# Two heads' score products as two row tiles of 64 in place of products over all 128 partitions, in a conditioned transformer block

## Chip, core and metric

One Trainium2 chip, one of its cores. The metric is the device time of the whole program in microseconds (us), here the median of three runs of the kernel before: 7162.6 us (7159.1 to 7167.75). Lower is better.

## What is computed

A transformer block on x [2, 2048, 576] with 16 heads of 36 features, all in float32. Cut to what matters here:

```python
mod = silu(c) @ w_ada + b_ada                    # six shifts, scales and gates
xn  = _ln(x, 1e-06) * (1 + sc_msa) + sh_msa
q, k, v = (xn @ w_qkv + b_qkv)                   # [2, 2048, 16, 36] each
q = _ln(q, 1e-05, qn_g, qn_b); k = _ln(k, 1e-05, kn_g, kn_b)
attn = softmax(einsum('bqhd,bkhd->bhqk', q, k) * 36 ** -0.5)
o = einsum('bhqk,bkhd->bqhd', attn, v)
x = x + g_msa * (o @ w_proj + b_proj)
x = x + g_mlp * (gelu(xn2 @ w1 + b1) @ w2 + b2)  # xn2: x normed and modulated again
```

## The kernel before, in words

Stages follow one another: modulation; then for each of the two batches `attention_inputs` (norm, q, k, v), `attention` and `projection`; then the MLP for both batches. The change lies in `attention`.

Attention works on pairs of heads. By `by_feature` (L309) four token tiles of a pair are copied by GpSimd into a staging tile (head 0 in columns 0 to 63, head 1 in 64 to 127, 36 of each used, the rest zero or a passing row), transposed by TensorE (L318, into the one PSUM tile `tp`), and written to SBUF by VectorE with gain and bias per partition (L322). So head 0 lies on partitions 0 to 35 and head 1 on 64 to 99. For k one tile `kt` [128, 2048] holds both heads. For q, `by_feature` writes two copies, `qt[:, 0]` with the gains "q0", which are zero on partitions 64 to 127, and `qt[:, 1]` with "q1", which are zero on 0 to 63: a product over all 128 partitions of `kt` and one of these copies is then one head's alone.

There are 64 steps to a pair (4 blocks of 512 queries by 16 key tiles of 128), and in each, in program order:

- **S**, `scores` (L361): for each head a matmul of keys [128] by queries [512] into its own bank of a two-bank PSUM tile `s`; ScalarE's exponential of both banks follows (L368);
- **M**, `largest` (L336), for the next pair: queries [128] by keys [512], again a bank for each head; VectorE reduces it to each query's largest score (L350). These maxima enter the next pair's S as one more row of q (`shifted_q`, L352) against a row of ones in k;
- **V**, `values` (L371), for the step before: two matmuls with 64 columns of v each, whose outputs take partitions 0 to 63 and 64 to 127 of one bank, `acc`.

**T** stands below for a group of four transposes (L318, or L387 in `finish`). Three `s` tiles of two banks, one `acc` and one `tp` fill PSUM's eight banks. Ahead of the loop stands a first round of 64 M alone for pair 0; pair 7's 64 steps have S and V alone. So the two batches hold 896 steps with S, M and V, 128 with S and V, and 128 M by themselves. The preparation of k and q for the pair after next runs in the last block of a pair (L422). The tile framework's scheduler sets each engine's final order from this program order.

In the profile each float32 matmul is two instructions (two passes, each with a weight load): the 2048 matmuls of L364 are 4096 rows.

The lines that the change touches: the gains (L95 to L109), `by_feature` (L309, L322), `prepare` (L332), `largest` (L343), `shifted_q` (L357), `scores` (L364).

## Time and profile before

| | |
|---|---|
| median of 3 runs | 7162.6 us (7159.1, 7162.6, 7167.75) |
| span of the profiled execution | 7159.0 us |
| the fastest run less that span | 0.1 us |
| TensorE busy | 6975.9 us, 97% |
| VectorE, ScalarE, GpSimd busy | 1964.8, 1441.5, 288.0 us |
| first M to last V of each batch, us of the span | 370 to 2844, 3262 to 5734 |
| MLP | from 5897 us to the end |

The profile is one execution. PE is TensorE's matmuls, PEld its weight loads, DVE is VectorE, ACT ScalarE, POOL GpSimd. The end of a matmul in the profile is modelled (a pass of 512 columns is shown as 592 ns while the next one starts 0.43 us after it), so distances between starts are read, not durations. [...]

### The profile page before, as it was taken

Reading aid. Unit: us, or ns where it says so; the run is one execution under the profiler, and the core shown is the slowest. Engines: PE = TensorE matmul, PEld = TensorE weight load, DVE = VectorE, ACT = ScalarE, POOL = GpSimd, SP = SyncE. Lnnn points to the kernel's source line nnn. Section 1 sums busy time; section 2 is a strip of 40 time slices with the busy share of each in tenths; the row PEclk is TensorE's granted clock in tenths of the full one; section 3 lists DMA queues with packets and bytes.
Section 4 is the critical chain, followed back from the end, with each engine's and each line's share of the span. In section 5 each row is a group of like instructions: output and inputs, shape, how many; then the busy total and the mean of one; then the engine's idle time right before and its main releaser. Section 6 shows DMA issues by size and latency. Waiting matters only on the chain.

```text
span 7159.0 us, 47198 instructions
## 1 busy us (share of the span) xinstructions
PE 6975.9 (97%) x20336; PEld 3021.2 (42%) x20336; DVE 1964.8 (27%) x2256; ACT 1441.5 (20%) x1789; POOL 288.0 (4%) x394
## 2 busy tenths in 40 slices
PE   8989999999999999998999999999999969999999
PEld 6643333333333333564333333333333345555555
DVE  3452333323233320346232333323332020000000
ACT  1102222222222223110222222222222311112110
POOL 0100000000000000110000000000000020000000
PEclk9989999999999999998999999999999989999999
DMA  2000000000000000200000000000000040000000
GB/s 94 5 0 0 0 0 0 0 0 0 0 0 0 0 0 21 90 7 0 0 0 0 0 0 0 0 0 0 0 0 0 1 143 14 14 14 14 15 15 10
DMA packets 35394, 83.60 MB, mean 12 GB/s; under 512 B 4833, under 2 KB 4833, under 8 KB 35185
## 3 DMA queue, kind: packets, MB, share of 16 engines
q1 hardware_dynamic: 29936, 61.69, 2.8%
q0 software_dynamic: 5248, 18.90, 0.7%
q8 instruction: 159, 2.61, 0.2%
q14 instruction: 51, 0.41, 0.0%
HBM read 61.68 MB, written 18.89 MB: 11 GB/s over the span
## 4 chain that ended last, share of the span: by engine, by line
PE 94%; issue 3%; DVE 1%; DMA 1%; ACT 0%; SPq 0%; POOL 0%; POOLq 0%; DVEq 0%; ACTq 0%
PE s L364 27%; PE s L343 25%; PE acc L374 14%; PE s L511 8%; PE s L249 7%; PE s L525 6%; PE s L449 3%; PE tp L318 2%; PE tp L209 1%; PE tp L387 0%; PE tp L138 0%; DMA x<-x_dram 0%; DVE qs L322 0%; DVE qt L322 0%; DMA xt<-in_x_dram 0%
## 5 line engine op out<-in xcount | busy, mean ns | idle before, releaser
L350 DVE TENSOR_REDUCE mx<-s 128x2 f32<-128x1024 f32 x1024 | 1255.3, 1226 | 2937.4 <-PE s L343 2937.1
L364 PE MATMUL s<-qs,kt 128*128 128x512 f32 x4096 | 2029.4, 618 | 14.5 <-DVE qs L322 14.5
L343 PE MATMUL s<-kt,qt 128*128 128x512 f32 x4096 | 1910.4, 593 | 1.9 <-issue 1.9
L368 ACT ACTIVATE pt<-s 128x1024 f32<-128x1024 f32 x1024 | 1047.7, 1023 | 3391.0 <-PE s L364 3391.0
L364 PEld LDWEIGHTS s<-qs,kt 128*128 128x128 f32 x4096 | 699.8, 190 | 1219.6 <-issue 1130.8
L343 PEld LDWEIGHTS s<-kt,qt 128*128 128x128 f32 x4096 | 780.3, 191 | 983.1 <-issue 972.6
L374 PE MATMUL acc<-pt,vt 128*64 128x512 f32 x4096 | 1104.4, 618 | 0.3 <-ACT pt L368 0.3
L511 PE MATMUL s<-xnt,w_sb 128*128 128x512 f32 (+1 forms) x1440 | 676.8, 613 | 0.3 <-ACT xnt L217 0.3
L525 PE MATMUL s<-w_sb,ht 128*128 128x288 f32 x2304 | 563.9, 406 | 0.0
L249 PE MATMUL s<-wq,xnt 128*128 128x288 f32 (+1 forms) x1920 | 543.3, 427 | 7.2 <-DMA wq<-in_w_qkv_dram 6.9
L374 PEld LDWEIGHTS acc<-pt,vt 128*64 128x64 f32 x4096 | 202.9, 135 | 741.3 <-issue 737.7
L525 PEld LDWEIGHTS s<-w_sb,ht 128*128 128x128 f32 x2304 | 435.4, 190 | 119.3 <-issue 1.5
L511 PEld LDWEIGHTS s<-xnt,w_sb 128*128 128x128 f32 (+1 forms) x1440 | 247.7, 189 | 421.0 <-issue 387.4
L249 PEld LDWEIGHTS s<-wq,xnt 128*128 128x128 f32 (+1 forms) x1920 | 334.2, 189 | 206.6 <-issue 142.8
L518 ACT ACTIVATE ht<-s,b_sb 128x512 f32<-128x512 f32 x144 | 98.9, 687 | 949.9 <-PE s L511 949.8
L533 DVE TENSOR_TENSOR y<-s,gate 128x576 f32<-128x576 f32 x32 | 24.2, 758 | 604.5 <-PE s L525 604.5
L449 PE MATMUL s<-wp,ott 128*128 128x288 f32 (+1 forms) x640 | 183.3, 429 | 0.7 <-DMA wp<-in_w_proj_dram 0.7
L322 DVE TENSOR_SCALAR qs<-tp,gain_q,bias_q 128x512 f32<-128x512 f32 x128 | 97.9, 806 | 295.9 <-PE tp L318 295.9
L313 POOL COPY stage_m<-qk 128x288 f32<-128x288 f32 x64 | 27.2, 427 | 3477.0 <-PE tp L318 3477.0
L202 DVE TENSOR_SCALAR xn<-x,mv,rstd 128x576 f32<-128x576 f32 x32 | 18.6, 585 | 491.9 <-PE acc L210 491.5
L449 PEld LDWEIGHTS s<-wp,ott 128*128 128x128 f32 (+1 forms) x640 | 113.1, 192 | 62.2 <-issue 39.9
L217 ACT ACTIVATE xnt<-tp,mod 128x128 f32<-128x128 f32 x256 | 99.1, 456 | 55.2 <-PE tp L209 54.9
(86 smaller groups left out, 1606.6 us busy)
## 6 DMA issues: line engine op xcount, KB each, us to landing
xt<-in_x_dram SPq DMA_DIRECT2D x64, 288.0 KB, 3.1
x_dram<-x POOLq DMA_DIRECT2D x32, 288.0 KB, 3.5
x<-x_dram SPq DMA_DIRECT2D x8, 1152.0 KB, 5.8
out_dram<-y POOLq DMA_DIRECT2D x32, 288.0 KB, 2.4
wa<-in_w_ada_dram SPq DMA_DIRECT2D x6, 1152.0 KB, 6.9
wq<-in_w_qkv_dram SPq DMA_DIRECT2D x6, 1152.0 KB, 11.7
w_sb<-in_w_dram SPq DMA_DIRECT2D x3, 1728.0 KB
w_sb<-in_w_dram SPq DMA_DIRECT2D x4, 1152.0 KB, 11.2
```

Of the source, the lines that this page charges most:

```text
L217: nc.scalar.activation(dst[:m, k, :], t4[:, k * P : (k + 1) * P] if k < 4 else t1[:64, :P], AF.Identity, bias=mod[:m, which, k, b : b + 1] ...
L249: nc.tensor.matmul(ps[:, a, :HALF], xnt[:kk, k, :], wq[:kk, k, f0 : f0 + HALF], start=(k == 0), stop=(k == NKC - 1),)
L318: nc.tensor.transpose(tp[:, i * P : (i + 1) * P], st[:, i].rearrange("p h e -> p (h e)"), ident)
L343: nc.tensor.matmul(ps[:, h, :], qts[p, blk][:, h, i * P : (i + 1) * P], kts[p][:, kq * BLK : (kq + 1) * BLK], start=True, stop=True,)
L350: nc.vector.tensor_reduce(maxima[p, blk][:, i, :, kq], ps, AX.X, ALU.max)
L364: nc.tensor.matmul(ps[:, h, :], kts[p][:, kc * P : (kc + 1) * P], qt[:, h, :], start=True, stop=True)
L368: nc.scalar.activation(pt, ps, AF.Exp, scale=SCALE)
L374: nc.tensor.matmul(acc[64 * h : 64 * h + 64, :], vt[:, v0 : v0 + 64], pt[:, h, :], start=(kc == 0), stop=(kc == NT - 1),)
L449: nc.tensor.matmul(ps[:, a, :HALF], ott[:kk, k, :], wp[:kk, k, a * HALF : (a + 1) * HALF], start=(k == 0), stop=(k == NKC - 1),)
L511: nc.tensor.matmul(ps[:, j, :], w1_sb[:kk, k, f * P : (f + 1) * P], xnt[:kk, k, :], start=(k == 0), stop=(k == NKC - 1),)
L518: nc.scalar.activation(ht[:, f, :], ps[:, j, :], AF.Gelu, bias=b1_sb[:, f : f + 1])
L525: nc.tensor.matmul(ps[:, a, :HALF], ht[:, f, i * P : (i + 1) * P], w2_sb[:, f, a * HALF : (a + 1) * HALF], start=(f == 0), stop=(f == NF - 1),
```

## The change

The second, masked copy of q is gone: gains and biases of q are one tile for both heads, like those of k; `by_feature` writes one tile with one VectorE instruction; `qt` and `qs` are [128, 512] in place of [128, 2, 512]. Each score product takes only its head's partitions, 36 (M) or 37 (S) of them from partition 0 or 64, and so uses a row tile of 64 of the matmul array. Number, columns and output banks of the matmuls stay.

```diff
-    for n, g_in, b_in, starts in (
-        ("k", kn_g, kn_b, (0, 64)),
-        ("q0", qn_g, qn_b, (0,)),
-        ("q1", qn_g, qn_b, (64,)),
-    ):
+    for n, g_in, b_in in (("k", kn_g, kn_b), ("q", qn_g, qn_b)):
...
-            def by_feature(n, p, blk, *normed):
+            def by_feature(n, p, blk, dst, g):
...
-                for dst, g in normed:
-                    nc.vector.tensor_scalar(dst, tp, gains[g], biases[g], ALU.mult, ALU.add)
+                nc.vector.tensor_scalar(dst, tp, gains[g], biases[g], ALU.mult, ALU.add)
...
-                    qt = b2p.tile([P, 2, BLK], F32, name="qt", bufs=5)
-                    by_feature("q", p, i - NBLK, (qt[:, 0, :], "q0"), (qt[:, 1, :], "q1"))
+                    qt = b2p.tile([P, BLK], F32, name="qt", bufs=5)
+                    by_feature("q", p, i - NBLK, qt, "q")
...
                 for h in range(2):
+                    r = slice(64 * h, 64 * h + HD)
                     nc.tensor.matmul(
                         ps[:, h, :],
-                        qts[p, blk][:, h, i * P : (i + 1) * P],
-                        kts[p][:, kq * BLK : (kq + 1) * BLK],
+                        qts[p, blk][r, i * P : (i + 1) * P],
+                        kts[p][r, kq * BLK : (kq + 1) * BLK],
...
-                qt = b2p.tile([P, 2, BLK], F32, name="qs")
-                by_feature("m", p, qb, (qt[:, 0, :], "q0"), (qt[:, 1, :], "q1"))
+                qt = b2p.tile([P, BLK], F32, name="qs")
+                by_feature("m", p, qb, qt, "q")
...
                 for h in range(2):
+                    r = slice(64 * h, 64 * h + HV)
                     nc.tensor.matmul(
-                        ps[:, h, :], kts[p][:, kc * P : (kc + 1) * P], qt[:, h, :], start=True, stop=True
+                        ps[:, h, :], kts[p][r, kc * P : (kc + 1) * P], qt[r, :], start=True, stop=True
                     )
```

Two places where the order of instructions moves. The first is VectorE at the start of a pair's second and third block (qs is the shifted q, L350 and L345 are the reductions behind M, L392 and L388 end `finish`). Before:

```order
L350 TENSOR_REDUCE mx<-s 128x2 x15
L322 TENSOR_SCALAR qs<-tp,gain_q_88,bias_q_89 128x512
L322 TENSOR_SCALAR qs<-tp,gain_q_95,bias_q_96 128x512
L354 TENSOR_REDUCE stage_m_1524<-mx 128x8
L350 TENSOR_REDUCE mx<-s 128x2
L390 RECIPROCAL inv<-tp 128x8
L392 TENSOR_TENSOR qk<-tp,inv 128x4x72
```

With the change:

```order
L345 TENSOR_REDUCE mx<-s 128x2 x15
L316 TENSOR_SCALAR qs<-tp,gain_q,bias_q 128x512
L349 TENSOR_REDUCE stage_m_1516<-mx 128x8
L345 TENSOR_REDUCE mx<-s 128x2
L386 RECIPROCAL inv<-tp 128x8
L388 TENSOR_TENSOR qk<-tp,inv 128x4x72
```

One of the two instructions that write qs is gone, and the others keep their order. The second place is TensorE at the start of the first round, where T for q and M alone alternate. Before:

```order
L318 MATMUL tp<-ident,stage_q_1520 128x128 x4
L343 MATMUL s<-kt,qt 128x512
L318 MATMUL tp<-ident,stage_q_1522 128x128 x4
L343 MATMUL s<-kt,qt 128x512 x3
L318 MATMUL tp<-ident,stage_q_1520 128x128 x4
L343 MATMUL s<-kt,qt 128x512 x4
L318 MATMUL tp<-ident,stage_q_1522 128x128 x4
L343 MATMUL s<-kt,qt 128x512 x120
```

With the change:

```order
L313 MATMUL tp<-ident,stage_q_1512 128x128 x4
L313 MATMUL tp<-ident,stage_q_1514 128x128 x4
L338 MATMUL s<-kt,qt 128x512 x2
L313 MATMUL tp<-ident,stage_q_1512 128x128 x4
L338 MATMUL s<-kt,qt 128x512 x2
L313 MATMUL tp<-ident,stage_q_1514 128x128 x4
L338 MATMUL s<-kt,qt 128x512 x124
```

A few M stand behind a T instead of ahead of it. Elsewhere TensorE's order of S, M, V and T is the one before.

## Rows read from the trace of the kernel before

**Rows 1.** The page: busy time, and the chain that ended last by engine and line

```profile
PE 6975.9 (97%) x20336; PEld 3021.2 (42%) x20336; DVE 1964.8 (27%) x2256; ACT 1441.5 (20%) x1789; POOL 288.0 (4%) x394
...
PE 94%; issue 3%; DVE 1%; DMA 1%; ACT 0%; SPq 0%; POOL 0%; POOLq 0%; DVEq 0%; ACTq 0%
PE s L364 27%; PE s L343 25%; PE acc L374 14%; PE s L511 8%; PE s L249 7%; PE s L525 6%; PE s L449 3%; PE tp L318 2%; PE tp L209 1%; PE tp L387 0%; PE tp L138 0%; DMA x<-x_dram 0%; DVE qs L322 0%; DVE qt L322 0%; DMA xt<-in_x_dram 0%
```

**Rows 2.** The page: groups of attention (count | busy us, mean ns | idle before, releaser)

```profile
L350 DVE TENSOR_REDUCE mx<-s 128x2 f32<-128x1024 f32 x1024 | 1255.3, 1226 | 2937.4 <-PE s L343 2937.1
L364 PE MATMUL s<-qs,kt 128*128 128x512 f32 x4096 | 2029.4, 618 | 14.5 <-DVE qs L322 14.5
L343 PE MATMUL s<-kt,qt 128*128 128x512 f32 x4096 | 1910.4, 593 | 1.9 <-issue 1.9
L368 ACT ACTIVATE pt<-s 128x1024 f32<-128x1024 f32 x1024 | 1047.7, 1023 | 3391.0 <-PE s L364 3391.0
...
L374 PE MATMUL acc<-pt,vt 128*64 128x512 f32 x4096 | 1104.4, 618 | 0.3 <-ACT pt L368 0.3
```

**Rows 3.** Timeline, weight loads of one step (start us, us, engine line op)

```profile
2002.47 0.20 PEld L374 LDWEIGHTS acc<-pt,vt 128*64 128x64 f32 x4 [0.76 <-issue]
2003.48 0.30 PEld L364 LDWEIGHTS s<-qs,kt 128*128 128x128 f32 x2 [0.81 <-issue]
2004.01 0.19 PEld L364 LDWEIGHTS s<-qs,kt 128*128 128x128 f32 x1 [0.24 <-issue]
...
2005.30 0.19 PEld L343 LDWEIGHTS s<-kt,qt 128*128 128x128 f32 x1 [0.24 <-issue]
...
2007.11 0.20 PEld L374 LDWEIGHTS acc<-pt,vt 128*64 128x64 f32 x4 [0.76 <-issue]
```

**Rows 4.** Timeline, weight loads of the MLP around a chunk of 64 rows

```profile
5903.61 0.29 PEld L511 LDWEIGHTS s<-xnt,w_sb 64*128 64x128 f32 x2 [0.76 <-issue]
5904.66 0.30 PEld L511 LDWEIGHTS s<-xnt,w_sb 128*128 128x128 f32 x2 [0.76 <-issue]
5905.20 0.19 PEld L511 LDWEIGHTS s<-xnt,w_sb 128*128 128x128 f32 x1 [0.24 <-issue]
```

**Rows 5.** Timeline, TensorE where T stands between M and S

```profile
1657.95 0.60 PE L387 MATMUL tp<-ident,ot 128*128 128x128 f32 x4
1658.39 1.88 PE L364 MATMUL s<-qs,kt 128*128 128x512 f32 x4
1660.11 0.59 PE L343 MATMUL s<-kt,qt 128*128 128x512 f32 x1
```

**Rows 6.** Timeline, ScalarE and VectorE in the step of rows 3

```profile
2005.56 1.02 ACT L368 ACTIVATE pt<-s 128x1024 f32<-128x1024 f32 x1 [3.62 <-PE s L364]
...
2007.22 1.23 DVE L350 TENSOR_REDUCE mx<-s 128x2 f32<-128x1024 f32 x1 [3.42 <-PE s L343]
```

**Rows 7.** Timeline, VectorE in batch 0's first round

```profile
380.07 2.52 DVE L350 TENSOR_REDUCE mx<-s 128x2 f32<-128x1024 f32 x2
...
386.95 1.23 DVE L350 TENSOR_REDUCE mx<-s 128x2 f32<-128x1024 f32 x1 [0.49 <-PE s L343]
...
395.54 1.23 DVE L350 TENSOR_REDUCE mx<-s 128x2 f32<-128x1024 f32 x1 [0.49 <-PE s L343]
```

**Rows 8.** Timeline, preparation of pair 1 behind that round

```profile
490.08 1.09 PE L318 MATMUL tp<-ident,stage_k 128*128 128x128 f32 x4 [1.00 <-DVE kt L322]
491.20 0.81 DVE L322 TENSOR_SCALAR kt<-tp,gain_k,bias_k 128x512 f32<-128x512 f32 x1 [1.27 <-PE tp L318]
...
493.22 1.53 DVE L322 TENSOR_SCALAR qt<-tp,gain_q,bias_q 128x512 f32<-128x512 f32 x2 [1.21 <-PE tp L318]
...
496.02 1.53 DVE L322 TENSOR_SCALAR qt<-tp,gain_q,bias_q 128x512 f32<-128x512 f32 x2 [1.27 <-PE tp L318]
```

**Rows 9.** Busy time by stretch: pair 1 and pair 7 of batch 0

```profile
812.30:1120.20 307.90, 305.29 (x832) 111.94 (x833) 96.69 (x96) 67.83 (x68) 5.13 (x12) 0.99 0.00 0
2652.00:2843.60 191.60, 190.53 (x538) 59.56 (x538) 8.30 (x16) 67.24 (x67) 0.85 (x2) 0.99 0.00 0
```

## The prediction

> **What bounds the kernel now.** The page comes first: TensorE is busy for 97% of the span and holds 94% of the chain that ended last; of that chain the two score products hold 27% (S) and 25% (M), and V 14% [rows 1]. VectorE and ScalarE wait for TensorE: before the 1024 reductions behind M VectorE is idle for 2937 us, before the exponentials ScalarE for 3391 us, while S waits 14.5 us in all and M and V almost nothing [rows 2]. So a step costs what TensorE needs for it.

> What it needs is read from the starts of the weight loads of one step [rows 3]. S starts at 2003.48, M at 2005.30, the next V at 2007.11; V had started at 2002.47. V takes 1.01 us, S 1.82, M 1.81, together 4.64 us. In the first round, where M runs alone, reductions start every (395.54 - 386.95) / 5 = 1.718 us for four passes [rows 7]; that is 0.43 us a pass, one slot below. So S is four slots and 0.10, M four and 0.09. V has four passes too, but takes 1.01 us, two slots (0.86) and 0.15: the four loads of both heads begin within 0.20 us (the row reads 0.20 us for x4), and the passes run two at a time, each head in its own 64 columns of the array. V shows that two float32 products in different parts of the array run side by side here, and that the second pass of one head does not hold up the first of the other.

> The fractions over are the price of changing the shape of the tile. [...] The same price stands at the MLP's chunk of 64 rows, the one place where a row tile of 64 already runs: two passes there take 5904.66 - 5903.61 = 1.05 us in place of 0.86, 0.19 over, and again 0.11 behind the return (5905.20 - 5904.66 = 0.54) [rows 4]. I take 0.20 us a change. Between T and S, both of 128 rows and columns, there is none: T takes 0.44 us, and S behind it 1.72, four bare slots [rows 5].

> **The change part by part.**

> *Full steps.* With head 0 in rows 0 to 63 and head 1 in rows 64 to 127, S and M run as V does, if row tiles behave as column tiles: eight passes in four slots. Each of the 896 full steps loses 4 x 0.4295 = 1.718 us, from 4.64 to 2.92; V and the two changes of shape stay. 896 x 1.718 = 1539 us.

> *Pair 7.* 128 steps of S and V lose two slots: 128 x 0.859 = 110 us. Its 64 steps now take 191.6 us a batch [rows 9].

> *First round.* M alone would fall from 1.718 to 0.859, but VectorE's reduction takes 1.23, and two in a row 2.52 us, so 2.52 - 1.23 = 1.29 from start to start [rows 7]. VectorE is late next: 1.718 - 1.29 = 0.43 gained for each of about 120 M (four in each batch stand among the T): 52 us. Were TensorE still the bound it would be 110.

> *VectorE.* The second copy of q goes: one instruction of 0.81 in place of two in 1.53 us [rows 8]. In the loop this is hidden before and after. In the preparation ahead of the loop TensorE waits for VectorE, groups of q follow every 496.02 - 493.22 = 2.80 us, and would follow 0.72 sooner: four groups in each batch for certain, some more in front of the first round; 8 us in all.

> *Changes of shape.* T is a tile of 128 by 128, so S no longer follows T for free: between V and S a T now costs one more change, between M and S two. In the order of the two programs TensorE changes shape 2044 times before and 2252 after: 208 x 0.20 = 41 us lost. [...]

> *What hides what, afterwards.* A step of 2.92 us holds 1.23 of VectorE and 1.02 of ScalarE [rows 6]. The exponential starts 0.26 us behind the start of M [rows 3, 6], which in the new step is at about 1.2, and ends 2.3 us into it; its V comes at 1.9 of the next step. The reduction of M ends some 1.3 us after V starts, at 3.2; the S that takes its two banks comes at 5.8. At a block's start qs is written beside V and is in time as now, since only its first half was waited for. Memsets and small loads at the program's start change in number by a few: nothing, they lie behind the modulation.

> *Sum.* 1539 + 110 + 52 + 8 - 41 = 1668. The span was 7159.0, so 5491; the median of the runs is 3.6 above that span, so **5494 us**. Pair 1 of batch 0, now 307.9 us [rows 9], should take 307.9 - 64 x 1.718 + 2.8 (14 changes) = 201.

> *Bounds.* No row shows two row tiles at work. If their first loads are made one after the other: 0.10 us for each of 1024 groups, +105. If each of the two tiles empties for itself when the shape changes: another 0.09, +92. If TensorE, now waiting a third of the time in the first round, is granted only half its clock there, as it is where T waits for VectorE (T takes 1.09 us at 490.08 against 0.60 [rows 5, 8]), M alone is 1.72 again: +52. Together 5743. From below: changes free within the 208 (-41) and the first round bounded by TensorE (-58): 5395. I keep the middle, since V does its two first loads together.

> **The rivals.**

> *The passes start in program order.* If a head's second pass must start before the other head's first one may, a run of S and M takes five slots in place of four, S and V of pair 7 three in place of two: 1024 x 0.43 = 440 us given back, 5930. Against it stands V, which under that order would be three slots, 1.44 us, and is 1.01 [rows 3]. For it: V's tiles share their rows, these do not. [...]

> *Row tiles take turns* (the other side: slower). Two row tiles would write all 128 partitions of two PSUM banks at once, where V's two tiles write 64 partitions each of one bank. If the array or its way out serves one row tile at a time, S and M keep eight slots, the step 4.64 us, and the 208 further changes are the price: 7159 + 41 - 8 = 7192, plus 3: 7195, 0.5% slower. It decides where less than 33 us of the 1668 are gained, 2% of the overlap. [...] For it: no row excludes it. Against it: V's overlap, with a clock of 0.99 in the stretch of a pair [rows 9].

> *The change does not make row tiles.* If a product over 36 rows from partition 64 were still given the full array, nothing would change but 0.8 us of VectorE, hidden. Against it: the MLP's product over 64 rows already pays a change of shape [rows 4]; the chance lies in "same".

> **How the numbers follow.** Overlap as in V: 0.84. Program order: 0.06. Taking turns: 0.09. No row tiles: 0.01. The predicted time is that of the first. Its bounds, 5395 to 5743, make the range 5390 to 5745 and hold 0.84 less a little for what is unknown in it; the two others need no place in it. Faster by over 0.2% (which is what a measurement of this kernel can tell from no change): 0.84 + 0.06 = 0.90. Slower: 0.09. Same: 0.01.

> **What would show it.** In the trace of the changed kernel: loads of S in pairs within some 0.2 us, as V's are now; V to V in 2.9 us; PE s of L338 and L360 at some half of their 2029 and 1910 us of busy time [rows 2]; reductions every 1.29 us in the first round, with VectorE never idle before them; pair 1 in 201 us; about 0.2 us more where S follows T. Wrong would be: V to V at 3.35 (program order), at 4.6 (turns), or a granted clock under 0.9 within a pair. VectorE or ScalarE named as what TensorE waits for in the loop would show that I missed a wait.

## The result, and the profile after

The changed kernel took 6036.36 us, the median of four runs (6014.04 to 6046.08); the kernel before, beside it, 7161.54. The ratio is 0.8425, with a 95% interval of 0.8407 to 0.8443. The sign was forecast; the time was not: 5494 was predicted, with a range of 5390 to 5745, and 542 us of the expected 1668 are missing.

The page of the changed kernel, lines that answer to [rows 1], and TensorE's granted clock in 40 slices of the span (PEclk, in tenths of full speed):

```profile
PE 5862.5 (97%) x20336; PEld 2405.9 (40%) x20336; DVE 1873.6 (31%) x2128; ACT 1441.3 (24%) x1789; POOL 288.1 (5%) x388
...
PEclk9965977997978899985898879779799899999999
...
PE 92%; issue 4%; DMA 1%; DVE 1%; SPq 0%; POOL 0%; ACT 0%; POOLq 0%; DVEq 0%; ACTq 0%
PE s L360 21%; PE acc L370 20%; PE s L338 19%; PE s L507 10%; PE s L244 9%; PE s L521 7%; PE s L445 3%; PE tp L313 2%; PE tp L204 1%; PE tp L383 1%; PE tp L133 0%; DMA x<-x_dram 0%; DVE qs L316 0%; DMA xt<-in_x_dram 0%; DMA wa<-in_w_ada_dram 0%
```

TensorE is still the bound, and no other engine has taken its place on the chain. What is new stands in the clock's line: many fives to eights in the slices of attention, a mean of 0.878 over the profiled execution.

The groups of attention, as in [rows 2]:

```profile
L360 PE MATMUL s<-qs,kt 37*128 37x512 f32 x4096 | 1332.6, 732 | 14.5 <-DVE qs L316 14.5
L338 PE MATMUL s<-kt,qt 36*128 36x512 f32 x4096 | 1310.4, 735 | 0.0
L370 PE MATMUL acc<-pt,vt 128*64 128x512 f32 x4096 | 1274.6, 705 | 0.7 <-ACT pt L364 0.7
```

V (L370), which the change does not touch, is busy for 1274.6 us where it was 1104.4 [rows 2]: whatever holds the kernel back also slows the stage that was left alone. S and M fell from 2029.4 and 1910.4 to 1332.6 and 1310.4, which is by less than half.

Now one step where the clock is whole, the weight loads as in [rows 3]:

```profile
2006.24 0.20 PEld L370 LDWEIGHTS acc<-pt,vt 128*64 128x64 f32 x4 [0.76 <-issue]
2007.25 0.30 PEld L360 LDWEIGHTS s<-qs,kt 37*128 37x128 f32 x4 [0.81 <-issue]
2007.79 0.19 PEld L338 LDWEIGHTS s<-kt,qt 36*128 36x128 f32 x2 [0.24 <-issue]
2008.22 0.20 PEld L338 LDWEIGHTS s<-kt,qt 36*128 36x128 f32 x2 [0.23 <-issue]
2009.17 0.20 PEld L370 LDWEIGHTS acc<-pt,vt 128*64 128x64 f32 x4 [0.76 <-issue]
```

From V to V it is 2.93 us; the prediction had 2.92. All four loads of S begin within the 0.30 us of one row, those of M two by two, 0.43 apart: the heads' row tiles run side by side, in float32, to the full. Where T stands between M and S, as in [rows 5], in the TensorE timeline:

```profile
2002.78 1.03 PE L338 MATMUL s<-kt,qt 36*128 36x512 f32 x4
2003.74 0.66 PE L383 MATMUL tp<-ident,ot 128*128 128x128 f32 x4
2004.33 1.13 PE L360 MATMUL s<-qs,kt 37*128 37x512 f32 x4
2005.29 1.03 PE L338 MATMUL s<-kt,qt 36*128 36x512 f32 x4
```

M takes 0.96 until T starts, T 0.59 in place of 0.44, S 0.96: some 0.35 us over the bare slots for two changes of shape; 0.40 was costed.

So a step at full clock is as predicted, and the time is lost in steps at half clock. Busy times by stretch of the changed kernel: block 0 of pair 1, its other three blocks, block 0 of pair 3 and the whole of pair 3, block 0 of pair 0, and a piece of the first round (the columns are those of [rows 9]: us, then busy us of PE, PEld, DVE, ACT and POOL with counts, then the granted clock, of which 1.00 is full speed):

```profile
745.50:834.00 88.50, 87.57 (x193) 23.76 (x193) 20.52 (x18) 16.37 (x16) 0.43 (x1) 0.51 0.00 1
834.00:987.40 153.40, 151.76 (x643) 49.57 (x641) 70.42 (x70) 51.46 (x52) 4.70 (x11) 0.99 0.00 0
...
1229.20:1276.40 47.20, 46.30 (x193) 14.52 (x193) 20.23 (x18) 16.37 (x16) 0.43 (x1) 1.00 0.00 1
...
1229.20:1428.50 199.30, 196.77 (x832) 63.66 (x833) 90.96 (x88) 67.83 (x68) 5.12 (x12) 1.00 0.00 1
...
502.80:592.50 89.70, 88.80 (x192) 24.25 (x192) 20.53 (x18) 17.65 (x17) 0.43 (x1) 0.50 0.00 0
...
375.00:480.00 105.00, 105.00 (x250) 42.02 (x248) 74.58 (x64) 0.00 (x0) 0.85 (x2) 0.50 0.00 0
```

Pair 3, at full clock throughout, takes 199.3 us; 201 were predicted. A pair's block 0 takes 47.2 us at full clock and 88.5 at half: 41.3 over. The trace's clock shows ten such blocks behind a pair boundary (five in each batch; the clock is down for 85 to 89 us each time), and two more in pair 0: 10 x 41.3 + 2 x 42.5 = 498. In the first round reductions come every 1.71 us:

```profile
399.35 1.23 DVE L345 TENSOR_REDUCE mx<-s 128x2 f32<-128x1024 f32 x1 [0.48 <-PE s L338]
401.06 1.23 DVE L345 TENSOR_REDUCE mx<-s 128x2 f32<-128x1024 f32 x1 [0.48 <-PE s L338]
```

Full clock, as the second experiment shows, would make that 1.13: 120 x 0.58 = 70 us. Together 568; and 6042.7 - 568 = 5475, where the prediction had a span of 5491.

Where does the clock fall, and where does it rise? TensorE's timeline at the start of pair 1, and at its second block:

```profile
743.91 0.66 PE L383 MATMUL tp<-ident,ot 128*128 128x128 f32 x4 [0.69 <-ACT ot L380]
745.52 0.63 PE L313 MATMUL tp<-ident,stage_m 128*128 128x128 f32 x4 [0.95 <-DVE qk L388]
747.06 1.26 PE L360 MATMUL s<-qs,kt 37*128 37x512 f32 x4 [0.91 <-DVE qs L316]
748.10 1.92 PE L338 MATMUL s<-kt,qt 36*128 36x512 f32 x4
...
833.95 1.12 PE L313 MATMUL tp<-ident,stage_m 128*128 128x128 f32 x4
835.00 1.90 PE L370 MATMUL acc<-pt,vt 128*64 128x512 f32 x4
836.82 0.70 PE L360 MATMUL s<-qs,kt 37*128 37x512 f32 x2
```

At the boundary TensorE waits three times (0.69, 0.95 and 0.91 us) for `finish` and the shifted q; S behind the last wait still takes 1.04 us, but M from 748.10 runs at half speed (1.92 for x4). It stays so, with TensorE busy all the while, for 88.7 us, and rises at the start of the next block, where T stands between two V. The kernel before had the same waits, here at the start of the same pair:

```profile
810.76 0.64 PE L387 MATMUL tp<-ident,ot 128*128 128x128 f32 x4 [0.71 <-ACT ot L384]
812.35 0.63 PE L318 MATMUL tp<-ident,stage_m 128*128 128x128 f32 x4 [0.96 <-DVE qk L392]
813.88 3.37 PE L364 MATMUL s<-qs,kt 128*128 128x512 f32 x4 [0.91 <-DVE qs L322]
817.09 1.88 PE L343 MATMUL s<-kt,qt 128*128 128x512 f32 x4
```

Its clock fell too: S behind the last wait is slow (3.37 against 1.88). But it rose again after 3.4 us, and M runs at full speed. In that trace it fell so at seven of the 14 boundaries (the expectation of e7, below, counts six): at the start of pairs 1, 3, 5 and 7 of the first batch and 2, 4 and 6 of the second.

In the changed kernel it fell at eleven of 14. The eleventh, at pair 7 of the second batch, where S and V run without M, was no long one. The clock was back after 10.2 us, in the steady run:

```profile
4479.46 3.79 PE L360 MATMUL s<-qs,kt 37*128 37x512 f32 x8 [0.90 <-DVE qs L316]
...
4488.99 1.13 PE L360 MATMUL s<-qs,kt 37*128 37x512 f32 x4
```

### The profile page after: what moved, and what is told of

It is laid out like the page before. It is cut to its first block, busy times and chain, and to the rows that moved or that the text cites. A ratio compares the mean times of both kernels' runs of the same rounds, so it can differ in the third digit from the quotient of the medians.

```text
span 6042.7 us, 47052 instructions
## 1 busy us (share of the span) xinstructions
PE 5862.5 (97%) x20336; PEld 2405.9 (40%) x20336; DVE 1873.6 (31%) x2128; ACT 1441.3 (24%) x1789; POOL 288.1 (5%) x388
## 4 chain that ended last, share of the span: by engine, by line
PE 92%; issue 4%; DMA 1%; DVE 1%; SPq 0%; POOL 0%; ACT 0%; POOLq 0%; DVEq 0%; ACTq 0%
PE s L360 21%; PE acc L370 20%; PE s L338 19%; PE s L507 10%; PE s L244 9%; PE s L521 7%; PE s L445 3%; PE tp L313 2%; PE tp L204 1%; PE tp L383 1%; PE tp L133 0%; DMA x<-x_dram 0%; DVE qs L316 0%; DMA xt<-in_x_dram 0%; DMA wa<-in_w_ada_dram 0%
## 5 line engine op out<-in xcount | busy, mean ns | idle before, releaser
L345 DVE TENSOR_REDUCE mx<-s 128x2 f32<-128x1024 f32 x1024 | 1255.7, 1226 | 1987.9 <-PE s L338 1987.9
L360 PE MATMUL s<-qs,kt 37*128 37x512 f32 x4096 | 1332.6, 732 | 14.5 <-DVE qs L316 14.5
L338 PE MATMUL s<-kt,qt 36*128 36x512 f32 x4096 | 1310.4, 735 | 0.0
L370 PE MATMUL acc<-pt,vt 128*64 128x512 f32 x4096 | 1274.6, 705 | 0.7 <-ACT pt L364 0.7
L338 PEld LDWEIGHTS s<-kt,qt 36*128 36x128 f32 x4096 | 489.2, 232 | 651.2 <-issue 648.9
L360 PEld LDWEIGHTS s<-qs,kt 37*128 37x128 f32 x4096 | 349.6, 208 | 893.5 <-issue 559.8
L370 PEld LDWEIGHTS acc<-pt,vt 128*64 128x64 f32 x4096 | 221.6, 148 | 878.6 <-issue 868.7
L316 DVE TENSOR_SCALAR qs<-tp,gain_q,bias_q 128x512 f32<-128x512 f32 x64 | 51.8, 810 | 238.4 <-PE tp L313 238.4
L272 ACT ACTIVATE sq<-qk 128x1152 f32<-128x1152 f32 x32 | 37.2, 1162 | 326.5 <-DVE qk L268 326.5
```

Of the source, the lines that this page charges most:

```text
L338: nc.tensor.matmul(ps[:, h, :], qts[p, blk][r, i * P : (i + 1) * P], kts[p][r, kq * BLK : (kq + 1) * BLK], start=True, stop=True,)
L345: nc.vector.tensor_reduce(maxima[p, blk][:, i, :, kq], ps, AX.X, ALU.max)
L360: nc.tensor.matmul(ps[:, h, :], kts[p][r, kc * P : (kc + 1) * P], qt[r, :], start=True, stop=True)
L370: nc.tensor.matmul(acc[64 * h : 64 * h + 64, :], vt[:, v0 : v0 + 64], pt[:, h, :], start=(kc == 0), stop=(kc == NT - 1),)
```

## The experiments

Three theories were tried. **A**: the clock falls in the wait between pairs, and the steady run of S, M and V in row tiles cannot raise it again. **B**: row tiles themselves make the chip hold the clock down, wherever they run. **C**, a refinement of A: it cannot rise because only 36 or 37 of each tile's 64 rows are given to the products. (By the short fall just shown, "cannot" is too strong for A and C alike: once in eleven times it did.)

**e1_joined**, the wait between pairs taken out: the last V and `finish` of a pair are issued behind the first S and M of the next.

```diff
+            behind = None
             for p in range(NPAIR):
-                behind = None
...
-                        values(p, *behind)
-                        if behind[2] == NT - 1:
-                            finish(p, qb - 1, behind[0])
+                        values(*behind)
+                        if behind[4] == NT - 1:
+                            finish(*behind[:3])
...
-                    behind = (acc, pt, kc)
+                    behind = (p, qb, acc, pt, kc)
...
-                values(p, *behind)
-                finish(p, NBLK - 1, behind[0])
+            values(*behind)
+            finish(*behind[:3])
```

> The changed kernel with the pairs joined: the last V and finish of a pair come behind the first S and M of the next, so that TensorE no longer waits some 2.6 us between pairs. Theory A (TensorE's clock falls in the wait between two pairs, and the steady run of S, M and V in row tiles cannot raise it again): no fall, or almost none, at the 14 pair boundaries; the ten stretches of half clock behind a boundary, 88.75 us each in place of some 47, go, which is 410 us, and up to 14 x 2.6 = 36 us of waiting: 5600 to 5640. Theory B (the row tiles themselves make the chip hold the clock down, wherever they run): the clock falls as often, 5980 to 6040. Both: the first rounds stay as they are.

Measured: 5598.77 us (5596.4 to 5600.3), ratio to the kernel before 0.782 [0.7809, 0.7832]. Pair 1 and the first round in its busy times by stretch:

```profile
742.90:940.70 197.80, 196.90 (x835) 63.54 (x833) 90.88 (x88) 67.83 (x68) 5.13 (x12) 1.00 0.00 1
```

```profile
375.00:480.00 105.00, 105.00 (x252) 41.93 (x250) 74.84 (x64) 0.00 (x0) 0.85 (x2) 0.50 0.00 0
```

No boundary lowers the clock any more, though one wait of 0.9 us is left at each; the same row tiles then run at 1.00 for pair after pair. That is as A expects (5600 to 5640 us), and B is out: products of 36 and 37 rows held a full clock here (1.00 over pair 1). The edit takes away two of the three waits and also moves the T of `finish` behind S and M; which of the two spares the clock was not separated. The first round, where nothing raised it, is still at 0.50, and there TensorE is busy for 105.00 of 105 us: it isn't waiting that keeps the clock down in this stretch.

**e2_rows64**, each product given all 64 rows of its tile. The rows from 37 on are zero in q and k; row 36 of k holds ones, against zeros of q in M. So the sums are the same.

```diff
-                    r = slice(64 * h, 64 * h + HD)
+                    r = slice(64 * h, 64 * h + 64)
...
-                    r = slice(64 * h, 64 * h + HV)
+                    r = slice(64 * h, 64 * h + 64)
```

> The changed kernel with all 64 rows of each row tile given to the products (64h to 64h+64) in place of 36 or 37; the further rows are zero in q or k, so the result stays. Waits and order stay. Theory C (the clock cannot rise because only 36 of 64 rows of each tile are at work): behind each boundary the clock returns within some 3 us as in the kernel before, the first rounds run at full clock, 5490 to 5560. Theory A without C, and theory B: no change, 6000 to 6050.

Measured: 5480.01 us (5476.33 to 5485.62), ratio 0.7657 [0.7645, 0.767]; 14 us from the number predicted for the change itself, and 10 under the 5490 to 5560 expected of this run. Its clock by slices, its start of pair 1 in TensorE's timeline, two V in succession, and its first round, as reductions and as busy times by stretch:

```profile
PEclk9999999999999999999999999999997999999999
```

```profile
668.57 0.63 PE L313 MATMUL tp<-ident,stage_m 128*128 128x128 f32 x4 [0.95 <-DVE qk L388]
670.10 1.58 PE L360 MATMUL s<-qs,kt 64*128 64x512 f32 x4 [0.90 <-DVE qs L316]
671.47 1.92 PE L338 MATMUL s<-kt,qt 64*128 64x512 f32 x4
673.17 1.47 PE L360 MATMUL s<-qs,kt 64*128 64x512 f32 x4
674.48 1.02 PE L338 MATMUL s<-kt,qt 64*128 64x512 f32 x4
...
999.93 1.08 PE L370 MATMUL acc<-pt,vt 128*64 128x512 f32 x4
...
1002.85 0.65 PE L370 MATMUL acc<-pt,vt 128*64 128x512 f32 x2
```

```profile
380.88 11.41 DVE L345 TENSOR_REDUCE mx<-s 128x2 f32<-128x1024 f32 x10
```

```profile
380.00:450.00 70.00, 69.28 (x252) 19.04 (x249) 69.76 (x65) 0.00 (x0) 0.34 (x1) 1.00 0.00 1
```

The waits are the same (0.95, 0.90) and the clock falls likewise (M at 671.47 takes 1.92), but during the next S it is back, and M at 674.48 takes 1.02; in the changed kernel that took until the next block. In the first round the clock stands at 1.00, and VectorE is the bound, as predicted, at (11.41 - 1.23) / 9 = 1.13 us a reduction. C holds: with the same waits at the boundaries and the same order and sums, 27 or 28 more rows, whose products are all zero, were worth 556 us. Whether some number of rows between 37 and 64 would do was not tried.

**e3_joined_rows64**, both edits:

> Both edits: pairs joined, and 64 rows. If C holds: 5450 to 5500, since the waits go too and the first rounds run at full clock. If only A holds: as with the pairs joined alone, 5600 to 5640. If B holds: 5980 to 6040.

Measured: 5442.48 us (5441.03 to 5443.63), ratio 0.7602 [0.7591, 0.7614], the fastest of all, 8 us under the range expected if C holds. Over e2 the joining saves 37.5 us. About 23 of them are the two waits that go at each of 14 boundaries (0.69 and 0.95 us; the one of 0.9 stays, as in e1), about 14 the half speed behind eight boundaries of e2's trace, 3.4 us long each. In the changed kernel the same edit saved 438.

**e4_dummy_t**, four transposes that nobody reads, behind the third step of each pair but the first:

```diff
+                    if p > 0 and qb == 0 and kc == 2:
+                        tp = tp_tile()
+                        for i in range(4):
+                            nc.tensor.transpose(tp[:, (i % 4) * P : (i % 4 + 1) * P], ident, ident)
```

> The changed kernel with four more transposes of the identity, whose output nobody reads, in the third step of the first block of each pair but the first. The clock was seen to return at the start of the second block, where transposes and two V stand close together. If the transposes raise it: the half clock behind a boundary ends some 15 us behind it in place of 88.75, saving some 34 us at each of ten boundaries, less 14 x 2 x 0.6 us for the transposes: 5700 to 5740. If they do not (the second V does, or something else): 6030 to 6060.

Measured: 5932.62 us, between the two answers, and far apart from run to run (5864.65, 5919.19, 5946.05 and 5993.82). Two boundaries of one execution, in TensorE's timeline (L418 are the added transposes):

```profile
760.76 0.94 PE L418 MATMUL tp<-ident 128*128 128x128 f32 x4
761.63 1.13 PE L360 MATMUL s<-qs,kt 37*128 37x512 f32 x4
...
1383.68 1.12 PE L418 MATMUL tp<-ident 128*128 128x128 f32 x4
1384.72 2.08 PE L360 MATMUL s<-qs,kt 37*128 37x512 f32 x4
```

At the first the clock rises among them and S behind them is fast (1.13); at the second they run at half speed and S stays slow (2.08). In this execution the clock fell at eleven boundaries; at five it was back after 10 to 17 us, during the added transposes or the S behind them, and at six it stayed down for the block. So the clock rose at the full-size transposes, or at the S behind them, at five of eleven boundaries, and not reliably (two of the five are in pair 7, where the changed kernel's clock came back once without them). What distinguishes the cases was not found.

**e5_s64** and **e6_m64**, 64 rows in one of the two products alone (one line of e2's edit each):

> The changed kernel with 64 rows in S alone; M keeps 36. With 64 rows in both it took 5480, with 36 and 37 rows 6036. If the rows of the products decide over the clock, the first round, which is M alone, stays at half clock (reductions every 1.72 us in place of 1.13, some 40 us more a batch). Behind the boundaries S and M run in turn: if S's rows suffice there, 5560 to 5600; if they don't, 5960 to 6040; if the clock comes back later than with both, between these. If rows are not what counts but some other effect of the full slices on M: as the changed kernel, 6000 to 6050.

> The changed kernel with 64 rows in M alone; S keeps 37. If rows decide, the first round runs at full clock (reductions every 1.13 us). Behind the boundaries: if M's rows suffice, 5480 to 5500; if they don't, 41 us for each of some ten boundaries, 5850 to 5900.

Measured: e5 5556.0 us (ratio 0.776 [0.7749, 0.7772]), e6 5525.94 us (0.771 [0.769, 0.773]; 5505.68 to 5539.63). First e5, a piece of the first round and the start of pair 3, where its clock falls, in two stretches; then e6, the same piece of the first round, pair 6, and the beginning of pair 7:

```profile
380.00:450.00 70.00, 70.00 (x165) 28.02 (x166) 50.46 (x44) 0.00 (x0) 0.43 (x1) 0.50 0.00 1
1106.50:1113.00 6.50, 6.46 (x16) 2.52 (x16) 1.31 (x2) 1.89 (x2) 0.00 (x0) 0.50 0.00 0
1113.20:1120.00 6.80, 6.80 (x30) 1.97 (x28) 3.04 (x3) 2.05 (x2) 0.00 (x0) 1.00 0.00 0
```

```profile
380.00:450.00 70.00, 69.29 (x250) 18.95 (x251) 69.78 (x65) 0.00 (x0) 0.43 (x1) 1.00 0.00 1
1672.60:1868.80 196.20, 193.66 (x801) 60.93 (x802) 84.45 (x80) 67.89 (x68) 1.71 (x4) 0.99 0.00 1
1868.80:1930.00 61.20, 60.30 (x128) 13.00 (x128) 0.90 (x2) 16.38 (x16) 0.43 (x1) 0.51 0.00 0
```

Where a stretch has one product with 64 rows, the trace's clock comes back within some 3 to 7 us of a pair boundary. Where none has, it stays down: in e5 the first round (M alone, 36 rows, 0.50), in e6 pair 7, which has no M and whose S has 37 rows (0.51 in the first batch; in the second the clock stays down there too, for 58 us). The first round of e6, where M waits for VectorE's reductions, has 1.00; that of e5, with no wait, 0.50. This ties the clock to the rows place by place, with one exception: in pair 7 of the changed kernel's second batch, with the same S and V as in e6, the clock came back after 10.2 us. My forecast for e6 (5480 to 5500) had left pair 7 out; that for e5 (5560 to 5600, if S's rows suffice) was 4 us too high.

**e7_before_joined**, the joining of e1 put into the kernel before:

> The kernel before, with the pairs joined as in the first of these runs, full products over 128 rows. There the clock fell at six boundaries for 3.4 us each only. If the wait between pairs is cheap by itself and dear only where the clock cannot come back: 14 x 2.6 + 6 x 1.7 = 47 us at most, 7110 to 7145. If the wait has a price of its own of the size that joining saved in the changed kernel (438 us): some 6720.

Measured: 7131.8 us, ratio 0.9962 [0.9949, 0.9975], 28 us. The wait is cheap in itself. It became dear in the changed kernel, where joining saved 438 us, because behind it the clock did not return for 85 to 89 us at ten boundaries.

## Why the prediction was wrong

**What held.** *Full steps*: eight passes in four slots, V to V 2.93 us against 2.92. *Changes of shape*: 0.35 us for the two around a T, against 0.40; the +92 of *Bounds*, for two tiles that each empty for themselves, was the author's estimate and is shown by no run. *Pair 1 at full clock*: 199.3 (read at pair 3) against 201. *First round*: VectorE is the bound at full clock, as e2 shows, at 1.13 us against the 1.29 taken; the two reductions of [rows 7], 2.52 us together, did not stand back to back without a wait for their data (0.08 us idle between them), so this term was put too low by some 20 us. In the changed kernel itself TensorE stayed the bound there, at half clock. *No new wait*: none of VectorE or ScalarE appeared in the loop. The whole sum, 5494, is close to what e2 takes (5480), where nothing but the rows given, and with them the clock, differs. Two small slips change nothing: 1024 x 0.10 is 102, not the 105 of *Bounds*, and the MLP is not the one place before with a row tile of 64 (L249 and L449 have such products too).

**Program order** and **taking turns**, the rivals, are excluded by the loads two by two and by 2.93 us. Program order would have made the step 3.35 if the four passes of a pair of heads stood head by head. In what order they stand in the program was not read.

**The step that failed** is *Bounds*, and in it the clock. I let it fall in one place, the first round, for 52 us, and elsewhere only among the signs of being wrong ("a granted clock under 0.9 within a pair"); against a fall in the loop I had "V's overlap, with a clock of 0.99 in the stretch of a pair". That row [rows 9] was of full products over 128 rows: it could not say what the clock does when 36 rows are given. And it begins with such a fall: its 0.99 is 3.4 us at half clock at the start of pair 1, in a stretch of 307.9. An outcome was missing between a full clock and half of it throughout: falls at the waits between pairs, already there in the trace of before at seven boundaries, that last a block of 88.7 us in place of 3.4 because the new steady state did not raise the clock in ten cases of eleven. Ten of those, two first blocks and two first rounds are the 568 us. With them the prediction's 5494 and the measured 6036 are accounted for to within 30 us.

Rows that were padding before may well not have been idle for the clock: the masked q of the kernel before gave each product 128 rows, most of them zero in q, and its clock returned some 3.4 us after each of the seven falls. The change took them away together with the second copy. That it was these rows in the kernel before is inferred from e2, e5 and e6, not shown by a run of its own.

What stays open: why the clock fell at eleven boundaries of 14 and not at all of them, why one of the eleven falls was short, and why the clock rose behind T at some boundaries of e4 only. And whether 36 rows without row tiles, one product at a time, would behave alike was not tried.

## What to carry to other kernels

Two row tiles of 64 ran two float32 products here in the slots of one (eight passes in four). Try giving each product all rows of its tile, zeros included: it cost nothing in the step here (2.93 us from V to V at full clock with 36 and 37 rows, 2.92 with 64) and was worth 556 us. When a change makes TensorE's work thinner, look at the granted clock of the stretch just behind each wait in the old trace, and ask what in the new kernel would raise it again; here the loop of 36 and 37 rows held 1.00 in e1 and stayed at 0.50 behind ten boundaries of the changed kernel. A wait on TensorE should then be priced with what follows it: the same joining, which takes away some 1.6 of the 2.6 us at a boundary, saved 2 us a boundary in the kernel before (28 / 14) and 31 in the changed one (438 / 14).
